# A listing that puts 64-row products behind each other: a three-line preference in the planner of a four-layer graph kernel, and a new order of all instructions

## The chip, the cores and the metric

The kernel runs on one core of one Trainium2 chip. The metric is the device time of the whole program in microseconds (us). Three runs of the kernel before were timed; their median is 1309.39 us, with 1308.24 and 1310.35 as the ends. The profile is of one execution on that core, taken by the hardware profiler.

## The reference

Four graph layers on 128 graphs of 64 nodes with 256 features, all float32. Each layer normalizes its input, applies relu, and adds its result to the input.

```python
x: (128, 64, 256)   adj: (128, 64, 64) of 0 and 1

# layer 0: attention with 4 heads; layer 1: the same with one head
h  = relu(layernorm(x))
Wh = h @ W                                   # 64 x 256 per graph
e  = leaky_relu(e_src[i] + e_dst[j]), masked by adj
x  = x + elu(softmax(e) @ Wh)

# layer 2: relations; adj holds only 0 and 1, so of 40 relations one is met
h  = relu(layernorm(x)); u = h @ W_loop.T; g = u @ Wg_loop.T
x  = x + relu(adj.T @ ((u + b) * sigmoid(g + bg)))

# layer 3: a gated recurrence, three steps
h  = relu(layernorm(x))
for i in range(3):
    a = adj.T @ (h @ weight[i])
    r, z = sigmoid(gates of a @ w_ih.T and h @ w_hh.T)
    n = tanh(a part + r * h part)
    h = (1 - z) * n + z * h
x  = x + h
```

## The kernel before

**Tiling.** Two graphs of 64 nodes make one tile of 128 rows; four such tiles make a group, and there are 16 groups. Each group passes through layer 0 (`attention` with 4 heads), layer 1 (`attention` with one head), layer 2 (`loop_relation`) and then the recurrence: `before_recurrence` makes its first state, and `Recurrence.step` is called three times. While one group is in the recurrence, later groups pass through the layers ahead of it.

**Two kinds of matmul.** Most products use all 128 rows of TensorE: features by features, with two groups of 128 features each. Products that follow the graphs' edges have 64 rows and 64 columns, since an edge never leaves its graph. `beside` records a whole set of those as one entry of the plan, with one cost, and marks it with `op.parts = True`. There are four kinds: 32 products for the edge sum of a recurrence step (`along`, banks tp and tq), 16 for two tiles of the first layer and 4 for two tiles of the second (`aggregate_graphs`, tiles wh and t), and 8 for the loop relation of a group (tiles v and oh; 4 where a group comes in halves). A float32 product of either kind is two passes in the profile; a transpose is one.

**The recurrence's products.** `Sevens` computes 256 outputs from 256 inputs in seven products of half size instead of eight; sums of the state (hS) and of the aggregated state (aS) are made on GpSimd (POOL). The products add up in banks named sy and sz (two of each), and between them ScalarE (ACT) or VectorE (DVE) read partial sums from the bank. So a product often has to wait until the last partial sum has been read.

**What sets the order.** Nothing runs when these functions are called. `Plan.note` records each instruction with a cost in nanoseconds. Then `emit` plans: `forward` places one instruction after another. At each turn it looks, for each engine, at the instructions whose inputs are there, keeps those that can start within `LEEWAY` of the earliest, and takes the one with the lowest due time. `backward` computes new due times from the end. After 40 passes (`PASSES`) with random noise (`SEED`), the best ranks are kept, and a list of numbered shifts (`MOVES`, each of which moves some jobs of one time window earlier or later on some engines) changes them. The last `forward` gives the order in which each engine's queue is written. A chip engine then follows its own queue in that order and waits where something isn't there.

`forward` already knows that two sets of 64-row products in a row are cheaper:

```python
if e == "PE":
    took -= self.TURN if op.parts and parts else 0.0
    parts = op.parts
```

`parts` says whether the last instruction on PE was such a set. Before the change it plays no part in which instruction is chosen.

**Fillers.** Up to 115 us of the plan, where PE would idle, the builder writes products on a constant tile (`warm`, into a bank sz that is not in use yet), as many as the planned gap takes.

**The last group's state.** For groups 0 and 15 (`PLAIN`) the first state is laid out otherwise. For group 15, `layernorm_T_by_dma` computes the statistics on DVE (bn_stats, bn_aggr), var and nm on ACT, rstd and nm on POOL, the normalized state hnat in four activations on ACT, a transposed copy tb in two DVE transposes, and then moves it with sixteen DMAs into hT. Nearly all DMAs are issued by SyncE's queue (SP), in their listed order; `back_by_dma` of another group shares that queue, with one DMA to way and four from way to hnat.

**General path.** Code for large attention weights is in the program behind a flag; with these inputs it isn't run.

Of the kernel before, what the change touches and what calls it, by code (L numbers as in the profile page):

```python
# [222 lines left out]
class Plan:  # L223
# [30 lines left out]
    def note(self, engine, call, cost, writes, reads, after=(), port=0.0, dma=False):  # L254
# [23 lines left out]
            b.ops.append(op)  # L278
        return op

    PASSES, SEED, SPREAD = 40, 36, 50.0
    MOVES = (
        4, 9, 10, 16, 23, 24, 27, 52, 54, 69, 126, 127, 131, 135, 153, 160, 168, 195, 197, 225, 228, 230, 231, 238,
        243, 259, 268, 282, 285, 293, 334, 352, 360, 378, 386, 388, 395, 403, 470, 495, 539, 546, 549, 581, 601, 638,
        801, 811, 868, 893, 987, 1041, 1080, 1096, 1098, 1213, 1245, 1316, 1336, 1486, 1497, 1582, 1605, 1616, 1655,
        1667, 1681, 1723, 1756, 1772, 1852, 1907, 1915, 1916, 1980, 1998, 2058, 2078, 2117, 2126, 2312, 2359, 2377,
        2491, 2542, 2642, 2735, 2796, 3084, 3324, 3575, 3667, 3804, 3814, 3827, 3910, 3929, 3954, 4282, 4343, 4403,
        4543, 4569, 4689, 4698, 5188, 5703, 5775, 5977, 6094, 6156, 6164, 6416, 6429, 6673, 6701, 6818, 6827, 6870,
        6877, 6914, 7169, 7256, 7306, 7435, 7462, 7518, 7538, 7777, 7800, 7818, 8187, 8200, 8201, 8220, 8241, 8356,
        8523, 8541, 8591, 8878, 8904, 9056, 9118, 9431, 9477, 9485, 9547, 9568, 9570, 9985, 10001, 10043, 10433,  # L290
        10478, 10511, 10525, 10621, 10791, 10884, 11083, 11298, 11321, 11366, 11841, 12653, 12716, 13557,
    )
    LEEWAY = {"PE": 100.0, "DVE": 100.0, "Activation": 100.0, "Pool": 100.0, "SP": 300.0, "-": 0.0}
    OVERLAP = {"DVE": 83.0, "Activation": 95.0, "Pool": 43.0}
    ISSUE, TURN = 665.0, 197.0

    def link(self):

# [31 lines left out]
    def forward(self):  # L330

        for b in self.bases:
            b.left, b.end, b.spot = len(b.ops), 0.0, None
        pools = {id(b.pool): b.pool for b in self.bases}.values()
        for pool in pools:
            pool.clear()
        for op in self.ops:
            op.job.left, op.waits = op.job.size, len(op.after)
        free = dict.fromkeys([*ENGINES.values(), "-"], 0.0)
        ready = {e: [] for e in free}  # L340
        held = {"DVE": 0.0, "Pool": 0.0}
        wire, parts = 2500.0, False
        order, self.replaced = [], []

        def enter(op):
            t = 0.0
            for other, data in op.after.items():
                late = other.end + self.LATENCY
                if other.engine == op.engine and not (other.dma and data):
                    late = other.start if op.engine in ("PE", "SP") or not data else other.end + 35.0  # L350
                if late > t:
                    t = late
            op.ready = t
            ready[op.engine].append(op)

        def spots(op, t):

            places = []
            for b in op.needs:
                if b.spot is None:  # L360
                    taken = [tag for x, tag in places if x.pool is b.pool]
                    tag = b.pool.place(b, taken)
                    if tag is None:
                        return None, t
                    places.append((b, tag))
                    t = max(t, b.pool.released(tag, b, taken.count(tag)))
            return places, t

        for op in self.ops:
            if not op.waits:  # L370
                enter(op)
        while len(order) < len(self.ops):
            best = None
            for e, ops in ready.items():
                leeway, first, found = self.LEEWAY[e], 1e18, []
                for op in ops:
                    t = op.ready if op.ready > free[e] else free[e]
                    if t > first + leeway or best is not None and t > best[0] + leeway:
                        continue
                    if any(j.left for j in op.job.after):  # L380
                        continue
                    places, t = spots(op, t)
                    if places is not None:
                        first = min(first, t)
                        found.append((t, op, places))
                found = [(t, op.due, op, places) for t, op, places in found if t <= first + leeway]
                if found:
                    found = min(found, key=lambda f: (f[1], f[0]))
                    if best is None or found[:2] < best[:2]:
                        best = found  # L390
            assert best is not None, "nothing can be emitted"
            t, _, op, op.places = best
            e = op.engine
            ready[e].remove(op)
            for b, tag in op.places:
                old = b.pool.put(b, tag)
                if old is not None:
                    self.replaced.append((old, op))
            if e == "-":
                for pool in pools:  # L400
                    pool.open = True
            op.start, op.idle = t, t - free[e]
            if op.dma:
                free[e] = t + self.ISSUE
                wire = max(wire, t + 1350.0) + op.cost
                op.end = wire + 400.0
            else:
                took = op.cost
# [3 lines that stand above are left out]
                elif op.port:  # L412
                    other = "Pool" if e == "DVE" else "DVE"
                    took = max(took, held[other] + min(op.port, took) - t)
                    held[e] = t + took
                op.end = t + took + (165.0 if e == "PE" else 0.0)
                free[e] = t + took - op.overlap
            for b in op.bases:
                b.left -= 1
                b.end = max(b.end, op.end)  # L420
            op.job.left -= 1
            order.append(op)
            for other in op.then:
                other.waits -= 1
                if not other.waits:
                    enter(other)
        return max(free.values()), order

    def backward(self, end):
# [10 lines left out]
        free = dict.fromkeys([*ENGINES.values(), "-"], end)  # L440
        ready = {e: [op for op in self.ops if op.engine == e and not op.waits] for e in free}
        for op in self.ops:
            op.took = min(op.end - op.start, 4500.0) if op.dma else op.end - op.start
            op.held = (op.took if op.engine in ("DVE", "Pool") else op.cost) - op.overlap
            if op.dma:
                op.held = self.ISSUE
            op.rank = op.end + self.random.gauss(0.0, self.SPREAD)

        def limit(op, late):
# [6 lines left out]
        for _ in self.ops:  # L456
# [6 lines left out]
            t, _, op = best  # L463
# [1422 lines left out]
```

## Time and profile before

| | |
|---|---|
| Median of three runs | 1309.39 us |
| The profiled execution's own time | 1310.08 us |
| Its span, first to last instruction | 1308.2 us |
| Mean granted TensorE clock | 0.996 |
| PE busy | 1289.3 us (99%), 9735 passes |
| DVE busy | 1051.5 us (80%) |
| ACT busy | 817.6 us (63%) |
| POOL busy | 708.1 us (54%) |
| DMA | 142.62 MB, 109 GB/s in the mean |
| PE's 64-row products: tp and tq | 55.1 us each, x1536 |
| PE's 64-row products: mm and mn of the first layer | 21.1 and 20.8 us, x496 each |

How to read it: the profile's lines name an instruction by line, engine, operation and tile, `out<-in`, with the buffers' numbers left out. Nearly all instructions have line 551, the helper that emits recorded ones; sets of 64-row products have line 841, in `beside`, and fillers line 1668. So one goes by the tiles' names. Matmuls are pipelined: the length of one is longer than its distance to the next, and the busy time of PE contains what happens between them. For what a product takes out of PE's time one looks at distances between starts.

### The profile page before, as it was taken

To read this page: it belongs to the slowest core of one execution; us is meant where nothing else is said; L and a number is where in the kernel's file an instruction comes from. 1 tells how busy PE (TensorE), PEld (TensorE's weight loads), DVE (VectorE), ACT (ScalarE), POOL (GpSimd) and SP (SyncE) were. 2 spreads that over 40 slices of the span, in tenths; PEclk is the share of its full clock that TensorE was granted. 3 is DMA by queue.
4 is the path that set the end of the run, shared out by engine and by line. 5 is a ranking of instruction groups with operands and counts; after the bars stand their busy time and mean duration, and the time that the engine had idled before them with its cause. 6 is when DMAs were issued, how large, how long until landed. Compare 5 with 4: busy or idle time off the path is not lost.

```text
span 1308.2 us, 27536 instructions
## 1 busy us (share of the span) xinstructions
PE 1289.3 (99%) x9735; PEld 1022.2 (78%) x9735; DVE 1051.5 (80%) x2536; ACT 817.6 (63%) x2095; POOL 708.1 (54%) x906
## 2 busy tenths in 40 slices
PE   9999999999999999999999999999999999999996
PEld 8667878788787877878787787878778788777885
DVE  7887869978789797987969788696978978875665
ACT  7866646666665665756666566756666666645543
POOL 4655535754455663655466456754655556455343
PEclk9999999999999999999999999999999999999998
DMA  8432223554555347454544654446634535232112
GB/s 234 78 51 49 69 70 90 157 115 130 100 164 104 113 109 147 122 109 135 122 106 101 140 144 95 139 102 121 146 98 139 113 102 120 74 87 72 58 66 68
DMA packets 306675, 142.62 MB, mean 109 GB/s; under 512 B 219616, under 2 KB 298976, under 8 KB 306528
## 3 DMA queue, kind: packets, MB, share of 16 engines
q1 hardware_dynamic: 305184, 140.50, 44.0%
q8 instruction: 79, 1.29, 0.4%
q14 instruction: 68, 0.56, 0.1%
q10 hardware_dynamic: 1344, 0.27, 0.1%
HBM read 78.39 MB, written 61.80 MB: 107 GB/s over the span
## 4 chain that ended last, share of the span: by engine, by line
PE 69%; DVE 12%; DMA 6%; ACT 4%; POOL 4%; issue 2%; SPq 2%; ACTq 0%; DVEq 0%; POOLq 0%
PE sy L551 28%; PE sz L551 21%; PE mm L551 14%; DVE hT L551 3%; PE mm L841 3%; PE tp L841 2%; DVE t L551 2%; ACT hn L551 2%; SPq L551 2%; DMA t<-row 2%; DVE r L551 1%; POOL xg L551 1%; DMA row<-fT 1%; DVE tb L551 1%; DVE st L551 1%
## 5 line engine op out<-in xcount | busy, mean ns | idle before, releaser
L551 POOL TENSOR_TENSOR r<-hT,hT 128x256 f32<-128x256 f32 x192 | 152.9, 805 | 272.1 <-ACT hT L551 270.6
L551 DVE SCALAR_TENSOR_TENSOR hT<-r,hT 128x256 f32<-128x256 f32 (+1 forms) x290 | 174.9, 610 | 25.3 <-ACT r L551 23.6
L551 PE MATMUL sz<-hS,whh 128*128 128x256 f32 x576 | 171.6, 383 | 2.3 <-DVE z L551 0.9
L551 PE MATMUL sy<-hS,wsum 128*128 128x256 f32 x576 | 172.2, 384 | 1.2 <-ACT r L551 0.9
L551 PE MATMUL sy<-aS,wsum 128*128 128x256 f32 x576 | 171.4, 381 | 0.0
L551 PE MATMUL sz<-aS,wc 128*128 128x256 f32 x576 | 170.2, 384 | 0.0
L551 DVE TENSOR_TENSOR hT<-hT,sz 128x256 f32<-128x256 f32 x288 | 118.3, 411 | 49.1 <-PE sz L551 44.3
L551 PEld LDWEIGHTS sy<-hS,wsum 128*128 128x128 f32 x576 | 106.9, 190 | 28.2 <-issue 6.7
L551 PEld LDWEIGHTS sz<-hS,whh 128*128 128x128 f32 x576 | 106.8, 190 | 27.2 <-issue 6.0
L551 PEld LDWEIGHTS sy<-aS,wsum 128*128 128x128 f32 x576 | 107.6, 190 | 23.3 <-issue 5.9
L551 ACT ACTIVATE hT<-hT,bi 128x256 f32<-128x256 f32 x192 | 94.8, 504 | 46.4 <-DVE hT L551 45.7
L551 ACT ACTIVATE hT<-sy,bh 128x256 f32<-128x256 f32 x192 | 90.4, 471 | 52.1 <-PE sy L551 48.5
L551 PEld LDWEIGHTS sz<-aS,wc 128*128 128x128 f32 x576 | 106.7, 190 | 20.3 <-issue 4.0
L551 PE MATMUL mm<-wl,hT 128*128 128x512 f32 x248 | 121.2, 594 | 0.0
L551 POOL TENSOR_TENSOR aS<-aT 128x256 f32<-128x256 f32 x96 | 78.4, 817 | 77.1 <-ACT aT L551 76.9
L551 ACT ACTIVATE hn<-xg,nm,rstd 128x256 f32<-128x256 f32 x200 | 108.5, 595 | 16.8 <-POOL nm L551 15.4
L551 ACT COPY z<-sy 128x256 f32<-128x256 f32 x192 | 70.0, 368 | 73.6 <-PE sy L551 72.8
L551 POOL TENSOR_TENSOR rstd<-var,mhalf 128x4 f32<-128x4 f32 (+1 forms) x70 | 79.7, 1139 | 58.9 <-ACT var L551 50.5
L551 DVE BATCH_NORM_STATS2 st<-xg 128x6 f32<-128x256 f32 x256 | 97.6, 411 | 11.6 <-POOL xg L551 8.3
L551 DVE TENSOR_TENSOR z<-sz,z 128x256 f32<-128x256 f32 x192 | 80.1, 417 | 26.6 <-PE sz L551 22.2
L551 DVE TENSOR_TENSOR hT<-hT,sy 128x256 f32<-128x256 f32 x192 | 79.8, 416 | 23.6 <-PE sy L551 21.5
L551 DVE SCALAR_TENSOR_TENSOR r<-z,r 128x512 f32<-128x512 f32 (+1 forms) x98 | 86.4, 887 | 10.8 <-POOL r L551 8.6
(211 smaller groups left out, 3155.5 us busy)
## 6 DMA issues: line engine op xcount, KB each, us to landing
way<-tb SPq DMA_DIRECT2D x59, 512.0 KB, 2.7
hnat<-way SPq DMA_DIRECT2D x184, 128.0 KB, 3.0
fine<-hn SPq DMA_DIRECT2D x168, 128.0 KB, 2.3
hT<-fine SPq DMA_DIRECT2D x84, 256.0 KB, 4.0
xg<-in_x_dram SPq DMA_DIRECT2D x15, 512.0 KB, 4.1
out_dram<-xg SPq DMA_DIRECT2D x15, 512.0 KB, 2.8
t<-row SPq DMA_DIRECT2D x28, 256.0 KB, 4.0
hT<-way SPq DMA_DIRECT2D x52, 128.0 KB, 3.7
```

The lines of the kernel that those rows point to most:

```text
L551: return do(*[real(a) for a in args], **{k: real(v) for k, v in kwargs.items()})
L841: nc.nc.tensor.matmul(*[real(x) for x in product], start=True, stop=True)
```

## The change

In `forward`, a set of 64-row products that could come right behind another such set gets its due time lowered by 1500 ns in the comparison. Two lines that price DMAs issued by GpSimd change their cost. A new seed and a new list of shifts give new ranks, and with them a new order of all instructions on all engines. The set of recorded instructions is the same.

```diff
-    PASSES, SEED, SPREAD = 40, 36, 50.0
+    PASSES, SEED, SPREAD = 40, 1, 50.0
     MOVES = (
-        4, 9, 10, 16, 23, 24, 27, 52, 54, 69, 126, 127, 131, 135, 153, 160, 168, 195, 197, 225, 228, 230, 231, 238,
...
+        11, 16, 22, 24, 28, 30, 34, 35, 40, 52, 58, 72, 89, 92, 94, 108, 125, 174, 179, 234, 242, 251, 278, 281, 285,
...
     )
     LEEWAY = {"PE": 100.0, "DVE": 100.0, "Activation": 100.0, "Pool": 100.0, "SP": 300.0, "-": 0.0}
     OVERLAP = {"DVE": 83.0, "Activation": 95.0, "Pool": 43.0}
-    ISSUE, TURN = 665.0, 197.0
+    ISSUE, TURN, JOIN = 665.0, 197.0, 1500.0
...
                     if places is not None:
                         first = min(first, t)
                         found.append((t, op, places))
-                found = [(t, op.due, op, places) for t, op, places in found if t <= first + leeway]
+                join = self.JOIN if e == "PE" and parts else 0.0
+                found = [
+                    (t, op.due - (join if op.parts else 0.0), op, places)
+                    for t, op, places in found if t <= first + leeway
+                ]
                 if found:
                     found = min(found, key=lambda f: (f[1], f[0]))
...
             if op.dma:
-                free[e] = t + self.ISSUE
+                free[e] = t + (1000.0 if e == "Pool" else self.ISSUE)
...
             if op.dma:
-                op.held = self.ISSUE
+                op.held = 1000.0 if op.engine == "Pool" else self.ISSUE
```

## The prediction

> **What bounds the kernel now.** I read the engines' busy time first, then the chain that ended last, then who TensorE (PE) waited for, then a table of stretches of the span.
>
> ```profile
> PE 1289.3 (99%) x9735; PEld 1022.2 (78%) x9735; DVE 1051.5 (80%) x2536; ACT 817.6 (63%) x2095; POOL 708.1 (54%) x906
> PE 69%; DVE 12%; DMA 6%; ACT 4%; POOL 4%; issue 2%; SPq 2%; ACTq 0%; DVEq 0%; POOLq 0%
> ```
>
> PE is in work for 99% of the span and holds 69% of the chain. Its waits, by what ended them (microseconds in total, times, longest), begin:
>
> ```profile
> PE tp L551 <- DVE hT L551: 2.3, 3, 1.3
> PE sy L551 <- DMA hnat<-way: 2.2, 1, 2.2
> PE sz L551 <- DVE z L551: 1.4, 4, 0.7
> ```
>
> These are small, so PE's own listing sets the time: a microsecond less on PE is a microsecond less of span, unless another engine is then late. By stretch (length; busy time of PE, PEld, DVE, ACT, POOL; granted clock; DMA):
>
> ```profile
> 130.00:1190.00 1060.00, 1055.61 (x7977) 839.14 (x7977) 872.83 (x2073) 666.52 (x1675) 580.02 (x712) 1.00 0.47 115
> 1190.00:1203.00 13.00, 10.85 (x104) 8.38 (x103) 7.83 (x15) 5.78 (x12) 8.09 (x11) 0.87 0.21 42
> 1290.00:1309.00 19.00, 8.07 (x36) 5.39 (x34) 10.43 (x23) 4.40 (x10) 5.92 (x6) 0.78 0.20 62
> ```
>
> But busy time hides the joints: matmuls overlap, so I price PE by the distance between starts. In the timeline a 256-column pass starts 0.216 us after the one before (two in 0.43), a 128-column one 0.11. The 64-row sets of L841 carry something more. Two second-layer sets that each stand alone, and then two that stand together (start, length, instruction):
>
> ```profile
> 596.70 0.59 PE L551 MATMUL sz<-aT,wc 128*128 128x256 f32 x2
> 597.13 0.59 PE L551 MATMUL sz<-hS,whh 128*128 128x256 f32 x2
> 597.65 0.43 PE L841 MATMUL mm<-wh,t 64*64 64x257 f32 x1
> ...
> 598.25 0.70 PE L551 MATMUL sz<-aS,wc 128*128 128x256 f32 x2
> 598.88 0.43 PE L841 MATMUL mm<-wh,t 64*64 64x257 f32 x1
> ...
> 599.47 0.70 PE L551 MATMUL sy<-aS,wsum 128*128 128x256 f32 x2
> 600.01 0.59 PE L551 MATMUL sy<-hT,wsum 128*128 128x256 f32 x2
> ```
>
> ```profile
> 204.78 0.59 PE L551 MATMUL sy<-hT,whh 128*128 128x256 f32 x2
> 205.31 0.43 PE L841 MATMUL mm<-wh,t 64*64 64x257 f32 x1
> ...
> 206.34 0.70 PE L551 MATMUL sy<-aT,wc 128*128 128x256 f32 x2
> 206.87 0.59 PE L551 MATMUL sz<-hS,whh 128*128 128x256 f32 x2
> ```
>
> Alone: 597.13 to 600.01 is 2.88 us; three pairs of 128-row passes in it take 3 x 0.43, so two sets cost 1.59. Together: 204.78 to 206.87 is 2.09; less 2 x 0.43 is 1.23. **Standing together saves 0.36 us**: one entry (0.09 us late), one exit (about 0.11), and a slow first 128-row pass behind it (0.70 for two instead of 0.59) are paid once. The same reckoning gives 0.356 for two first-layer sets (0.823 alone, 1.290 together), 0.343 for an edge sum with a first-layer set.
>
> [...]
>
> ```profile
> 1183.61 10.63 SPq L551 DMA_DIRECT2D hT<-tb  x16
> 1194.28 2.29 SPq L551 DMA_DIRECT2D hnat<-way  x2
> ```
>
> ```profile
> 1197.63 1.58 PE L551 MATMUL sy<-hT,whh 128*128 128x256 f32 x4 [2.15 <-DMA hnat<-way]
> 1199.01 1.06 PE L551 MATMUL sy<-aT,wc 128*128 128x256 f32 x2
> 1199.86 1.85 PE L551 MATMUL sz<-hT,whh 128*128 128x256 f32 x4
> ```
>
> The last group's state goes through sixteen DMA issues in a row; PE waits 2.3 us by starts, then runs its passes 0.43 us apart for about 4 us. This spot costs 4.2 us.
>
> **The account of before.** PE's listing, each pass at its own spacing and each of the 113 spells in 64-row mode at 0.356, adds up to 1267.7 us. The last product starts at 1300.5, so 32.8 us are lost: 10.4 up to 130 us (of it 1.1 before the first pass and 2.9 for passes at half clock), 13.4 in 130 to 1190 in some thirty waits of 0.03 to 0.8 us, each with a slow pass of 0.1 behind it, 4.2 at 1197, 0.5 up to 1290, 3.9 in the last ten microseconds. Behind the last product stand 7.7 us (last additions, output DMAs, closing): 1308.2, the span. The profiled execution took 1310.08, 1.9 around the span; the median of the three is 1309.39. I take differences from the account and set them on the median.
>
> **The change, part by part.** Numbers of instructions per engine are the same in both listings, but for fillers.
> - *Joins.* 130 executed 64-row sets, in 113 spells before and 105 after. Pairs of second-layer sets stay at 10; pairs of first-layer sets go from 2 to 7; the other joins are mixed. 8 x 0.356 = **-2.85 us**. Ends: 8 x 0.343 = -2.74 and 8 x 0.358 = -2.86.
> - *Fillers (warm).* 35 before, 37 after; 17 instead of 13 stand ahead of the first transposes. Thirteen took 1.06 to 6.77, and the clock rose then, so four more are 8 passes at 0.11: +0.9 there, given back as later groups have fewer. Two more in all: +0.44 if nothing was awaited there, 0 if they fill waits. VectorE's statistics and the normalized tile lead to the products behind them, so I take 0; ends -0.5 and +0.9.
> - *Waits for a partial sum* (a product returns to a bank whose last sum ScalarE or VectorE reads first). Returns within 1.3 us of PE work: 294 before, 311 after. In the trace 11 of 297 such returns stalled, 3.7 us together, so 17 more cost 17 x 3.7/297 = +0.2. But the whole 13.4 us is made anew by another order: thirty events of about 0.4 us with a scatter as large as their mean give 0.4 x sqrt(60), about 3 us either way for two orders. Taken +0.2.
> - *The last group's state.* The sixteen issues still stand between the second and third part of an hnat load, and the PE work from the group's last loop product to the first use is the same (22.0 us). On VectorE one gate product (0.6) now stands behind the statistics rather than ahead: -0.6. On POOL an aS difference (0.82) now stands between rstd and nm, and ScalarE's r of the next step stands behind the four hnat activations with two copies: VectorE's transposes, queued behind that step's product, can be 0.4 to 1.2 later. SP's sixteen issues and then PE wait for these. Taken 0; ends -1.0 and +1.2.
> - *The end.* VectorE's first output addition (0.68) moves ahead of the last gate product: the first output DMA goes 0.3 earlier, the last transposes 0.7 later; the third DMA, issued at 1302.24 behind two others, finds its data at about the same time. 0.
> - *The planner's 1000.0 for POOL's DMAs*: no DMA stands on POOL, so it moves nothing.
> Sum: -2.85 + 0 + 0.2 + 0 + 0 = -2.65. Span 1305.5, median **1306.7 us**.
>
> **Rivals.**
> 1. *The new order also waits less* (0.24). For: new sz tiles that take a bank within 1.5 us of its last product fall from 56 to 48 (of sy they rise from 64 to 68), and with 13.4 us in small waits there is room. Against: returns to partial sums are as tight as before. A third of 13.4 less: -2.65 - 4.5 = 1302.2.
> 2. *The gain is taken by waits that follow* (0.20). PE comes 0.36 us sooner after each join, and whoever feeds it does not; VectorE, 80% busy, is next. Then about 1309.4. Against: the sixteen joins already there show no wait of that size behind them but for two.
> 3. *Slower* (0.12): the last group's sixteen DMAs. Each microsecond that the group's statistics, nm or transposes come later is one of PE[...]. It decides from 5.3 us of extra lateness, the 2.65 and the bound of 2.6; with 6 us, 1312.8. Against: the orders there differ by 1.2 at most.
> 4. *The change does nothing*: pairs would have been made anyway. The listing has 8 spells fewer, so only placement luck would be left; this lies within 2.
>
> **How the numbers follow.** The likeliest case (0.44) is joins paid and waits as before, 1306.7, its own range 1304 to 1309.4. About 0.2% (2.6 us) is what a measurement of this kernel can tell from no change: faster is below 1306.8, slower above 1312.0. The likeliest case straddles the first bound; I put 0.28 of its 0.44 below, 0.14 within and 0.02 above the second, since the head and the small waits have more room to fall than my terms use. Rival 1 gives 0.24 faster, rival 2 0.02 faster, 0.02 slower and 0.16 same, rival 3 0.12 slower. Faster 0.24 + 0.28 + 0.02 = 0.54; slower 0.12 + 0.02 + 0.02 = 0.16; same 0.14 + 0.16 = 0.30. Eight in ten: from 1301.0 (most of rival 1, a head that gains 0.5) to 1311.2 (rival 2 and the upper ends of the head and the last group), leaving about 1 in 10 on either side.
>
> **What would show it.** Right: 105 spells in the timeline of PE, joined first-layer sets at about 1.29 us, PE waits from 130 to 1190 us again near 13 us, the wait for the last group's state at 1.5 to 3.5 us in the stretch that is now 1190 to 1203, the rest unchanged. Wrong: lone sets at another price; a new wait of over 2 us with half clock behind it; a head whose first layer is done over 1 us sooner or later; or a wait of the last group beyond 5 us.

## The result, and the profile after

The changed kernel takes 1304.39 us (1301.53 to 1305.48, six runs) where the kernel before takes 1309.45 (1308.24 to 1310.35, six runs). The ratio is 0.996, 95% interval 0.9949 to 0.9972: 5.1 us less, between 3.7 and 6.7. The forecast was 2.65 less, 1306.7. The direction and the range held; the size was half of what was measured, and lies below the interval.

The first page of the profile after, engines and chain of waits:

```profile
PE 1285.1 (99%) x9739; PEld 1021.6 (78%) x9739; DVE 1059.2 (81%) x2536; ACT 818.5 (63%) x2095; POOL 720.9 (55%) x906
PE 65%; DVE 9%; POOL 9%; ACT 6%; DMA 5%; issue 3%; SPq 2%; ACTq 0%; DVEq 0%; POOLq 0%
```

PE is still the bound. Four more passes are the two more fillers. Who PE waited for (total, times, longest):

```profile
PE tp L556 <- DVE hT L556: 2.6, 4, 1.3
PE sz L556 <- DVE z L556: 2.1, 2, 1.5
PE sy L556 <- DMA hT<-tb: 1.7, 1, 1.7
```

No wait is new in kind. The wait for the last group's state is 1.7 instead of 2.2; why the profile names another DMA for it than before is told further down, under the reasons. The stretches (length; busy time of PE, PEld, DVE, ACT, POOL; granted clock; DMA):

```profile
130.00:1190.00 1060.00, 1054.25 (x7984) 841.38 (x7982) 882.09 (x2075) 668.48 (x1679) 589.46 (x712) 1.00 0.47 115
1190.00:1203.00 13.00, 11.19 (x167) 9.13 (x167) 9.24 (x18) 6.86 (x15) 10.44 (x13) 1.00 0.21 43
1290.00:1309.00 19.00, 5.28 (x22) 3.01 (x20) 7.52 (x17) 2.75 (x7) 3.54 (x5) 0.75 0.19 60
```

In the second line the clock stays at 1.00, where it was 0.87 before. A joined pair of first-layer sets in PE's timeline, with the 128-row products around it (the other 62 rows of the 64 in between left out):

```profile
312.95 0.59 PE L556 MATMUL sz<-aS,wc 128*128 128x256 f32 x2
313.47 0.27 PE L846 MATMUL mm<-wh,t 64*64 64x65 f32 x1
...
314.42 0.22 PE L846 MATMUL mn<-wh,t 64*64 64x65 f32 x1
314.57 0.70 PE L556 MATMUL sy<-aT,wsum 128*128 128x256 f32 x2
315.10 0.59 PE L556 MATMUL sy<-aS,wsum 128*128 128x256 f32 x2
```

From 312.95 to 315.10 are 2.15 us; two pairs of 128-row passes take 0.86 of it, so the two sets cost 1.29. All seven such pairs cost 1.289 to 1.290, lone sets 0.823 in the middle, and PE's timeline has 105 spells of 64-row products. That part of the forecast came true to the hundredth.

**The account made again.** "Listing" is PE's order priced as in the prediction; "lost" is how much later than that price a product starts, here by stretch of the span (the borders are times in each row's own profile). "Behind it" is the time from the start of the last product to the end. Each row adds up to 0.2 to 0.3 less than its span. The second profile of each kernel is from two of the experiments, which ran it unchanged once more.

| profile | listing | lost to 130 us | 130 to 1185 | 1185 to 1203 | 1203 to 1285 | 1285 to the last product | behind it | span |
|---|---|---|---|---|---|---|---|---|
| before | 1267.74 | 10.4 | 13.6 | 3.8 | 0.7 | 4.0 | 7.7 | 1308.2 |
| before, again | 1267.74 | 10.0 | 14.6 | 2.3 | 0.7 | 4.2 | 7.5 | 1307.3 |
| after | 1265.33 | 10.2 | 15.2 | 2.3 | 0.0 | 4.3 | 6.1 | 1303.7 |
| after, again | 1265.33 | 9.3 | 14.7 | 4.0 | 0.0 | 4.1 | 6.3 | 1303.9 |

Means of the two: span -3.95, of it listing -2.4 (joins -2.85, two fillers +0.44), to 130 us -0.5, the long middle +0.8, the last group +0.1, behind it -0.7, the end from 1285 on -1.3. The timed difference is larger than that of the profiles partly because the profiled execution after, 1305.48, is the slowest of its six, while the one before, 1310.08, is 0.6 above its median.

### The profile page after: what moved, and what is told of

Its sections match the earlier page's. It is cut to its first block, busy times and chain, and to the rows that moved or that the text cites. A ratio compares the mean times of both kernels' runs of the same rounds, so it can differ in the third digit from the quotient of the medians.

```text
span 1303.7 us, 27568 instructions
## 1 busy us (share of the span) xinstructions
PE 1285.1 (99%) x9739; PEld 1021.6 (78%) x9739; DVE 1059.2 (81%) x2536; ACT 818.5 (63%) x2095; POOL 720.9 (55%) x906
## 3 DMA queue, kind: packets, MB, share of 16 engines
q8 instruction: 79, 1.29, 0.4%
## 4 chain that ended last, share of the span: by engine, by line
PE 65%; DVE 9%; POOL 9%; ACT 6%; DMA 5%; issue 3%; SPq 2%; ACTq 0%; DVEq 0%; POOLq 0%
PE sy L556 26%; PE sz L556 19%; PE mm L556 14%; ACT hn L556 3%; DVE hT L556 2%; PE mm L846 2%; PE tp L846 2%; POOL xg L556 2%; SPq L556 2%; POOL r L556 2%; POOL hS L556 2%; DVE r L556 2%; POOL aS L556 1%; DMA way<-tb 1%; DMA row<-fT 1%
## 5 line engine op out<-in xcount | busy, mean ns | idle before, releaser
L556 POOL TENSOR_TENSOR r<-hT,hT 128x256 f32<-128x256 f32 x192 | 163.4, 862 | 238.6 <-ACT hT L556 234.3
L556 PEld LDWEIGHTS sy<-hS,wsum 128*128 128x128 f32 x576 | 105.7, 190 | 32.6 <-issue 6.7
L556 POOL TENSOR_TENSOR aS<-aT 128x256 f32<-128x256 f32 x96 | 83.5, 870 | 76.2 <-ACT aT L556 76.2
L556 POOL TENSOR_TENSOR rstd<-var,mhalf 128x4 f32<-128x4 f32 (+1 forms) x70 | 75.3, 1076 | 85.8 <-ACT var L556 81.2
L556 DVE SCALAR_TENSOR_TENSOR r<-z,r 128x512 f32<-128x512 f32 (+1 forms) x98 | 91.3, 936 | 11.3 <-POOL r L556 10.5
```

Of the source, the lines that this page charges most:

```text
L556: return do(*[real(a) for a in args], **{k: real(v) for k, v in kwargs.items()})
```

## Experiments

Three theories stand in the first two expectations. A is the forecast's: a spell less is 0.356 us less, and the waits stay as they are. B: the gain comes from the new order and not from its joins. C is the forecast's second rival: PE comes sooner and waits longer, so that joins pay little. Differences are taken to the kernel before on the same chip: 1310.27 for the first four, 1309.34 for the next four, 1308.89 for the last two.

### 1. The order of before, with joins put in by hand

```diff
+        best = best[0], self.together(best[1])
```

This takes the finished order of before and moves one to three 128-row products that stand between two 64-row sets ahead of or behind the pair, where nothing that they need or feed is passed. The rest of PE's order, and all other queues, stay. 113 spells become 100.

> The kernel before with its own seed, shifts and planned order; only afterwards, where one to three 128-row products stand between two 64-row sets, they are moved ahead of or behind the pair. 100 spells in 64-row mode instead of 113. Theory A (a join is worth 0.356 us wherever it is made): 13 x 0.356 = 4.6 us less than before, 1304.8. Theory B (the gain of the change comes from the new order, not from its joins): within 1 us of before, 1308.5 to 1310.5. Theory C (each join is paid back by a wait behind it): 1307 to 1309.

Measured: 1312.97 us (1309.27 to 1316.06, 22 runs), ratio 1.0022 (1.0014 to 1.003): 2.7 us *slower*, though its listing is 4.63 shorter. By the account 39.1 us are lost at the last product instead of 32.6, and the surplus of 7 to 8 us stands in the middle (21.7 from 130 to 1185). PE's waits in that kernel begin:

```profile
PE sz L607 <- DVE z L607: 2.6, 5, 0.6
PE tp L607 <- DVE hT L607: 2.3, 3, 1.3
```

That is slower than any of the three theories said (1304.8, 1308.5 to 1310.5, 1307 to 1309). Taken alone it looks like C and more. But two things were changed: sets were joined, and products left the places for which VectorE's and ScalarE's queues had been laid out. Experiment 6 parts the two, in part.

### 2. The changed kernel, with its pairs split

```diff
+        best = best[0], self.apart(best[1])
```

In the order of after, the next 128-row product that is free to go there is put between two sets that stand together: 129 spells instead of 105.

> The changed kernel with its own planned order; only afterwards, one 128-row product is put between two 64-row sets wherever it is free to go there. 129 spells instead of 105, so 24 more entries. Theory A: 24 x 0.356 = 8.5 us more than the changed kernel, about 1313. Theory B: within 1 us of the changed kernel. Theory C (a set that is split also gives the other engines 0.4 us more to read): 4 to 6 us more.

Measured: 1313.78 us (1310.12 to 1318.12, ten runs), ratio to before 1.0027 (1.0012 to 1.0041). The changed kernel itself, on the same chip, took 1305.84 (experiment 4): 7.9 us for 24 spells, 0.33 each. By the account the listing is 8.55 longer and only 0.4 to 0.5 more is lost. The pair shown above is now two sets with one product between:

```profile
314.95 0.59 PE L605 MATMUL sz<-aS,wc 128*128 128x256 f32 x2
315.47 0.27 PE L895 MATMUL mm<-wh,t 64*64 64x65 f32 x1
...
316.10 0.70 PE L605 MATMUL sy<-aT,wsum 128*128 128x256 f32 x2
316.73 0.27 PE L895 MATMUL mm<-wh,t 64*64 64x65 f32 x1
...
317.36 0.70 PE L605 MATMUL sy<-aS,wsum 128*128 128x256 f32 x2
317.89 0.59 PE L605 MATMUL sz<-aT,wc 128*128 128x256 f32 x2
```

From 314.95 to 317.89 are 2.94 us, of which three pairs of 128-row passes are 1.29: 1.65 for the two sets, where together they cost 1.29. Theory A holds in this direction, with nothing of it hidden; B (within 1 us of the changed kernel) and C (4 to 6 us more) do not.

### 3 and 10. The last group's sixteen DMAs on two queues

```diff
-                    nc.sync.dma_start(to, of[:, :, j * S : (j + 1) * S])
+                    by_two_queues(to, of[:, :, j * S : (j + 1) * S], (i + j) % 2)
```

The listing is the changed kernel's, but every second of the sixteen is issued by ScalarE, at the place in ScalarE's order at which it comes in the listing.

> The changed kernel in its own order; of the sixteen DMAs that move the last group's first state, every second one is issued by ScalarE's queue instead of SP's. If PE's wait for the last of them (1.9 us by starts in the profile of the changed kernel) is due to sixteen issues in a row on SP, SP is done 5 us sooner, the wait goes, and the time falls by 1.5 to 2 us, by 3 to 4 where the clock had been halved behind it. Rival: eight issues on ScalarE hold up what it reads for PE, and the time stays within 1 us or rises by up to 4.

> The changed kernel with two queues again, since its first profile (1303.6 us of span) was no shorter than that of the changed kernel (1303.7) while its timed median was 3.1 us lower. If the timed gain is real, its ratio to before is again 0.993 to 0.995, against 0.996 to 0.997 of the changed kernel. If the profile tells the truth, the ratio is 0.996 or above.

Measured: 1302.76 us (1301.17 to 1305.41, five runs), ratio 0.9937 (0.9924 to 0.995); on another chip 1303.2 (1301.77 to 1305.58), ratio 0.9963 (0.9949 to 0.9978). The sixteen issues in the timeline of SP after, and then the eight that are left to it in experiment 3:

```profile
1183.57 11.19 SPq L556 DMA_DIRECT2D hT<-tb  x16
```

```profile
1184.55 5.78 SPq L811 DMA_DIRECT2D hT<-tb  x8
1193.29 0.59 ACTq L811 DMA_DIRECT2D hT<-tb  x1
1196.34 1.10 PE L556 MATMUL sy<-hT,whh 128*128 128x256 f32 x4 [0.61 <-DMA hT<-tb]
```

PE waits 0.61 us (0.34 in experiment 10) instead of 1.72, and the clock isn't halved behind it; in the table's stretch from 1185 to 1203 they lose 1.2 and 1.0 us, against 2.3 and 4.0 in the two profiles of the changed kernel. So the spot is worth 1 to 3 us and can be had. As a whole kernel these are the shortest times seen. Against the changed kernel the first chip gives 3.1 us less; on the second only the ratio to before can be set beside the changed kernel's 0.996 and 0.9967, and there is no gain beyond the intervals (the expectation took 0.996 or above as a sign of no gain; it is 0.9963). By the times the gain isn't settled; by the profiles the spot is repaired.

### 4 and 5. Both kernels once more

No edit.

> The changed kernel unchanged, for a second profile and its scatter. If what differs between its runs (1301.5 to 1305.5) is the halved clock or the wait at the last group, this profile's stretch from 1190 to 1203 us differs from the first by about as much as its span does. If it is the small waits between 130 and 1190 us, the lost time there differs by that instead. If it is the closing after the last product, the part behind the last product differs (6.1 us in the first profile, 7.7 in that of before).

> The kernel before unchanged, for a second profile. Its first has 7.7 us behind the last product, the changed kernel's two have 6.1 and 6.3. If VectorE's order at the end makes that difference, this profile shows 7.5 or more again; if the slow issue of the last two output DMAs (0.88 and 1.41 us) was chance, it shows 6.5 to 7. The time is that of before within 0.2%, and lost time up to the last product 32 to 34 us.

Measured: after 1305.84 us (1304.56 to 1307.47, five runs), ratio 0.9967 (0.9954 to 0.9979); before 1309.08 (1307.16 to 1311.43, 13 runs), ratio to itself 1.0001 (0.9993 to 1.001). The gain repeats, 4.4 us. The two profiles are in the table above, and show how far two executions of one program differ: those of after differ by 1.7 us in the stretch of the last group, and by 0.2 in the span. The product that waits for the last group's state, after and after again:

```profile
1196.47 1.10 PE L556 MATMUL sy<-hT,whh 128*128 128x256 f32 x4 [1.72 <-DMA hT<-tb]
1197.41 0.59 PE L556 MATMUL sy<-aT,wc 128*128 128x256 f32 x2
```

```profile
1195.08 1.72 PE L556 MATMUL sy<-hT,whh 128*128 128x256 f32 x4 [1.72 <-DMA hT<-tb]
1196.60 1.06 PE L556 MATMUL sy<-aT,wc 128*128 128x256 f32 x2
```

The same wait of 1.72 us; in one execution full clock behind it, in the other half clock for 3.4 us, which costs 1.7. Of the two profiles of before, too, one has the half clock (the one shown in the prediction, behind a wait of 2.15 us; 0.87 in the mean from 1190 to 1203) and one hasn't (behind 2.22 us; 1.00). So the clock of 1.00 in the window of after is no gain of the change: executions of one program differ in it. The length of the wait alone doesn't decide it, and what does isn't shown.

### 6. The control of experiment 1: the same products moved, the sets not joined

The edit is shown against experiment 1:

```diff
-        best = best[0], self.together(best[1])
+        best = best[0], self.filled(self.together(best[1]))
```

Each pair that experiment 1 makes gets another 128-row product between its sets: 112 spells, as many as before but for one.

> A control for the run in which the pairs of the kernel before were joined by hand (100 spells, 39.1 us lost instead of 32.6): the same 128-row products are moved, but another 128-row product is then put between the two sets of each pair, so that 112 spells stay. If the waits of that run came from PE being 0.36 us ahead of its feeders at each join, they go: 32.5 to 34.5 us lost, 1309 to 1312. If they came from products moved out of the order that the other engines' queues follow, they stay: 37 to 40 us lost, 1314 to 1317.

Measured: 1315.24 us (1314.62 to 1315.41, five runs), ratio 1.0045 (1.0031 to 1.0058): 5.9 us slower than before, with a listing only 0.4 shorter. Lost at the last product: 39.2, the 39.1 of experiment 1. Its longest waits:

```profile
PE sz L635 <- DVE z L635: 5.1, 7, 1.5
PE tp L635 <- DVE hT L635: 2.3, 3, 1.3
```

So a loss of seven microseconds comes without the joins too, from products moved against queues that stay as they were. It is not all the same loss. Between 130 and 1180 us, 23 passes of experiment 1 wait over 0.15 us beyond their price where neither profile of before shows such a wait, 8.1 us together; in experiment 6 it is also 23, with 8.8 us. Ten of them, 4.2 and 4.8 us, are of the same products in both. For this half joins aren't the cause, and theory C is excluded. The other half stands elsewhere in the two runs, and the control moves twelve products of its own, so for that half it is not. If the disturbance is taken as equal in both, the 12 joins are worth 5.9 - 2.7 = 3.2 us, 0.27 each; the listings give 4.3. Each of the two differences is known to 1 to 2 us, so 0.356 isn't excluded, nor is some loss.

### 7 and 8. The preference and the new numbers, each alone

Experiment 7 is the changed kernel with the seed and shifts of before; experiment 8 is the changed kernel with

```diff
-    ISSUE, TURN, JOIN = 665.0, 197.0, 1500.0
+    ISSUE, TURN, JOIN = 665.0, 197.0, 0.0
```

> The change's preference with the seed and the shifts of before, all planned anew: 107 spells (6 fewer, -2.1 us) and 41 fillers (6 more, at most +1.3). If the preference alone makes the gain, 1307.5 to 1309 on a before of 1310, with 32 to 33 us lost. If the shifts only fit the order that they were listed with, lost time rises to 35 to 42 and the run is slower than before, 1312 to 1319.

> The change's seed and shifts without its preference (the 1500 is zero), all planned anew: 119 spells (14 more than the changed kernel, +5.0 us) and 43 fillers (6 more, at most +1.3). If the new numbers make the gain by fewer waits, lost time stays at 32 and the run is 5 to 6 us above the changed kernel, 1311 to 1312. If the shifts only fit the order that they were listed with, lost time rises too, to 35 to 42: 1314 to 1322.

| | spells | fillers | listing | lost at the last product | time | ratio to before |
|---|---|---|---|---|---|---|
| before | 113 | 35 | 1267.74 | 32.6 | 1309.45 | |
| 7, preference alone | 107 | 41 | 1266.92 | 75.4 | 1348.13 (five runs) | 1.0293 (1.0279 to 1.0307) |
| 8, numbers alone | 119 | 43 | 1271.64 | 53.3 | 1334.88 (five runs) | 1.0206 (1.0192 to 1.022) |
| after, both | 105 | 37 | 1265.33 | 32.0 | 1304.39 | 0.996 (0.9949 to 0.9972) |

What PE waited for in experiment 7, and then in 8:

```profile
PE sz L555 <- DVE hT L555: 7.0, 10, 1.6
PE sy L555 <- ACT r L555: 6.8, 8, 1.6
```

```profile
PE sy L556 <- ACT r L556: 5.1, 8, 2.2
PE sy L556 <- DMA hT<-tb: 3.5, 1, 3.5
```

Neither part alone is an improvement, and both are far slower than was expected even for shifts that do not fit (1312 to 1319, and 1314 to 1322). The listings are at most 4 us longer than that of before, as the spells and fillers say; the losses are 21 and 43 us larger. The likely reading is that a list of shifts fits only the order that it was made with, and that another order loses tens of microseconds in small waits for VectorE and ScalarE; two runs show it, no more. With the new numbers the preference removes 14 spells (119 to 105), but what it is worth alone can't be read from 8 against after, where the waits change by more.

### 9. The kernel before, with two queues

The edit is that of experiment 3, in the order of before.

> The kernel before in its own order, with every second of the last group's sixteen DMAs issued by ScalarE's queue. In its two profiles the spot costs 4.0 us (clock halved behind the wait) and 2.4 (not halved). If the issues on SP are the cause in this order too, the time falls by 2 to 4 us against before. If what ScalarE reads is held up instead, it stays within 1 us.

Measured: 1307.24 us (1305.23 to 1309.74, 21 runs), ratio 0.9988 (0.9981 to 0.9995): 1.65 less, below what was expected. SP's and the last of ScalarE's issues, and the product that waits:

```profile
1182.58 5.93 SPq L806 DMA_DIRECT2D hT<-tb  x8
1192.37 0.59 ACTq L806 DMA_DIRECT2D hT<-tb  x1
1196.22 1.10 PE L551 MATMUL sy<-hT,whh 128*128 128x256 f32 x4 [1.76 <-DMA hT<-tb]
```

SP is done by 1188.5, but ScalarE issues its last one only at 1192.37, behind work of its own, and the product starts 3.3 us after that issue ends. Counted from the first of the sixteen, the last issue ends after 10.4 us, where it took 10.6 on SP alone: half of the DMAs came little sooner by going to ScalarE. The 3.3 us behind it are a late landing, which the next section takes up. The loss in the table's stretch is 1.9; it was 3.8 with the half clock and 2.3 without.

## Why the prediction was right, and where not

- *Joins, -2.85.* Right. 105 spells, the price to the hundredth, and splitting them again costs 0.33 each in the time (experiment 2). This is the largest term of the gain.
- *Fillers, 0.* The two more are +0.44 in the listing; the loss up to 130 us falls by 0.5 in the mean. But the head also varies from one execution to the next: full clock is reached at 6.9 and 5.4 us before, 6.0 and 4.2 after. Zero is what the runs allow to say.
- *Waits for partial sums and the middle, +0.2 with a scatter of 3.* From 130 to 1185 +0.8 in the mean; the two executions of before differ by 1.0 there, and experiments 3 and 10, one program, by 2.9 (16.1 and 13.2). The size can't be told from chance. The stretch 1203 to 1285, where the prediction had 0.5 in its account and changed nothing, lost 0.7 in both profiles before and nothing in both after: a small gain of the new order that no term held. Most of it is one wait of 0.5 us with its slow pass, at 1223.54 in before, which experiments 1 and 9 have too. The profile counts 0.2 of it (first line below), and for after it shows no wait of PE there. PE's waits from 1203 to 1290 us in before, and one from 1285 to 1302 that the end needs:

```profile
PE sz L551 <- DVE hT L551: 0.2, 1, 0.2
PE sz L551 <- DVE z L551: 0.3, 1, 0.3
```

- *The last group's state, 0.* Right in the mean (+0.1), partly by luck. The largest effect there is whether the clock halves, and the wait itself is not only the sixteen issues. In before PE waits for the sixteenth transfer and not for the load of hnat that the profile names: that transfer raises its semaphore for the last time at 1197.29, PE's wait for this semaphore ends at 1197.32, and its wait for the semaphore that the load of hnat uses takes 0.05. From issue to landing the sixteenth takes 3.7 us in before, 2.0 in after, and 3.7 for the last of experiment 9. The lines are of the fifteenth and sixteenth together in before, then of the last in after and in experiment 9:

```profile
DMA to landing us min/median/max: 2.0/2.8/3.7
DMA to landing us min/median/max: 2.0/2.0/2.0
DMA to landing us min/median/max: 3.7/3.7/3.7
```

  It is 3.8 in before again and 3.7 in experiment 1; in after again and in experiments 2 and 6 it is 2.0. So of the 2.3 us by starts in before some 1.7 is a late landing, and of the 1.9 in after 0.6 is one slow issue among the sixteen (1.24 instead of 0.61). Without either, an estimate from these figures, PE would have waited 0.6 before and 1.3 after: the new order would be 0.7 later there, within the 0.4 to 1.2 that the prediction allowed for VectorE's transposes, and the two delays hid it. That it is the transposes isn't shown.
- *The end, 0.* This step failed in its size. From 1285 on the kernel is 1.3 us shorter in both profiles. The prediction said that the last transposes come 0.7 later, and the first output DMA 0.3 earlier. Counted from the first transpose of the end, the traces give 0.6 later and 0.3 earlier: the order did as foretold. What was taken as given is the length of the output DMAs' issues. SP's timeline at the end, before and then after:

```profile
1300.82 2.83 SPq L551 DMA_DIRECT2D out_dram<-hnat  x3
```

```profile
1296.86 1.97 SPq L556 DMA_DIRECT2D out_dram<-hnat  x3
```

The last two issues took 0.88 and 1.41 us before (0.89 and 1.40 in the second profile), and 0.37 each after (0.37 and 0.53). It isn't VectorE's order that makes them slow, since experiment 9 has the order of before there:

```profile
1297.80 1.49 SPq L551 DMA_DIRECT2D out_dram<-hnat  x3
```

From the first transpose of the end to the last instruction experiment 9 takes 9.22, as the changed kernel does (9.18 and 9.29), against 10.08 in both profiles of before. Experiment 5 had taken a second 7.5 behind the last product, which came, as a sign of VectorE's order; with experiment 9 it is none. So 0.85 of the 1.3 goes with two slow issues that both profiles of before have; in all other kernels run here they took 0.37 to 0.77. What is known of such issues stands in the last section; the cause is open. The other 0.45 is one wait for z ahead of the last products (second line of the waits above): by starts, with the slow pass behind it, 0.6 and 0.7 us before, 0.3 and 0.1 after.

- *Rival 1, fewer waits.* Not so in the middle; the two short stretches behind it carry 2.0 of the 4.5 us that it hoped for. *Rival 2, the gain taken by waits.* False for the planned order (experiment 2). What looked like it in experiment 1 came by about half from moved products (experiment 6); the other half is open. *Rival 3, the last group.* The wait grew in no profile of the changed kernel: 1.72 twice. *Rival 4.* Excluded by the 105 spells; experiment 8 shows 119 without the preference.
- *Two sums of the prediction.* Its parts of the lost time add up to 32.4 us, not 32.8. The entry, exit and slow pass that it names add up to 0.31; the 0.36 of a spell was measured as a whole, and holds as a whole.

In sum: -2.4 by the listing as forecast within the fillers, -1.3 at the end and -0.7 behind the last group that were not in the sum, +0.4 for the rest, -4.0 in the profiles. The times say -5.1 and -4.4; the remainder is within their intervals, and within what one program varies.

## What to carry to other kernels

Price a change of order on a TensorE that is busy for 99% of the span by distances between starts: what a spell of 64-row products costs beyond its passes doesn't show in busy time (PE counts as busy for all of the 2.88 us of the prediction's two lone sets and all of the 2.09 us of its joined ones), and its 0.36 us held between starts in both directions, and in the time where pairs were split (0.33). Joins paid here in the order whose queues were all planned with them, and did not where products were moved afterwards past queues that stayed; a control that moves work too shows how much of the loss comes from the moving, if one looks whether it falls on the same products. A sum over the bound engine sizes what was meant, but tens of microseconds sit in small waits and in the two ends (32.6 lost up to the last product and 7.7 behind it in before): list those stretches one by one, and look at two executions of one program before putting a microsecond down to a change.

## What was not expected of the hardware

**The issue and the landing of one DMA vary by a microsecond and more.** Most issues of a kind take the same time: of the 52 from way to hT in the kernel after, the median is 0.43 us, but the longest took 1.73. Of 850 or 858 issues on SP in each profile, 54 to 72 took over 0.6 us longer than the shortest of their kind. Most are the same ones in two executions of a program: 54 of the 61 in before are slow again in before again, 46 of the 57 in after.

A late landing makes the longest of the waits for z. VectorE and PE in after, and then in after again:

```profile
513.78 1.30 DVE L556 STREAM_TRANSPOSE tb<-hnat 128x512 f32<-128x512 f32 x2 [1.11 <-DMA way<-tb]
526.29 0.42 DVE L556 TENSOR_TENSOR t<-t,gd 128x256 f32<-128x256 f32 x1 [1.94 <-DMA t<-row]
526.63 0.42 DVE L556 TENSOR_TENSOR z<-sz,z 128x256 f32<-128x256 f32 x1
527.11 0.70 PE L556 MATMUL sz<-aT,wc 128*128 128x256 f32 x2 [1.52 <-DVE z L556]
```

```profile
511.65 1.29 DVE L556 STREAM_TRANSPOSE tb<-hnat 128x512 f32<-128x512 f32 x2
524.11 0.43 DVE L556 TENSOR_TENSOR t<-t,gd 128x256 f32<-128x256 f32 x1 [0.70 <-DMA t<-row]
524.45 0.42 DVE L556 TENSOR_TENSOR z<-sz,z 128x256 f32<-128x256 f32 x1
524.92 0.70 PE L556 MATMUL sz<-aT,wc 128*128 128x256 f32 x2 [0.27 <-DVE z L556]
```

PE's products ahead of this stand 0.93 us later in after than in after again (522.38 and 521.45 for the same one), so the rest of each difference is lateness. A transfer from tb to way, issued at 509.12, lands after 4.6 us; in after again it takes 3.2. Of its sixteen signals fifteen are there by 511.82, the last at 513.69. VectorE's transposes of hnat wait for it and are 1.2 us late. The issues on SP behind them stay late, VectorE's first use of t is 1.25 us late, and z, which needs nothing of that transfer but stands behind in VectorE's queue, makes PE wait 1.52 instead of 0.27. In between one issue on SP takes 1.70 instead of 0.42, and the transfer to row for which t waits in its turn lands after 3.7 us instead of 2.2; they are not what decides, since the transposes ahead of them are late by nearly as much as t. In after all 2536 operations of VectorE start in the order in which the program lists them, by the names of the tiles they write; none passes another that waits. In experiments 3 and 10, again one program, the same transposes wait 1.27 us for the same transfer in one, and not in the other. The profile names VectorE as the one waited for; the cause lies 13 us back, at a landing.

Slow issues and late landings have a companion in the traces. Each profile lists 79 packets of 16 KB as queue 8, kind "instruction", of about 1.1 us each. Of the 68 issues that are slow in only one execution of a program (before with before again, after with after again, experiment 3 with 10), 59 overlap such a packet; of the issues that are not slow, 4 to 6% do. A packet lies between issue and landing of the late transfer to way (509.97 to 511.55 in after; the one of after again begins before the issue) and of the late sixteenth transfer (1194.77 to 1196.19 in before), and on the last output DMA's slow issue in both profiles of before (from 1301.89 and 1301.31; in after it comes 0.6 us behind that issue). This is a coincidence in time and not a shown cause: of the same 68 issues, 31 overlap a packet also in the execution where they are not slow.

**The clock at half after a short wait** came in three of the profiles that have a wait of 1.6 to 2.2 us at the last group (before, after again, experiment 2), and not in four others (before again, after, experiments 1 and 9). Each time it lasted 3.4 us. Experiment 8 has it for 3.4 us behind its wait of 3.5. Experiment 7, with its many waits, has three stretches of half clock, one of 3.4 and two of 6.8 us.
